# A pre-norm decoder layer on one core: the second chunk of tokens is loaded right behind the keys' weights, and products of ones stand between the last two steps of the maxima's lead

## The chip, the cores and the metric

The kernel runs on one NeuronCore of a Trainium2 chip. The metric is the device time of one execution in microseconds (us); lower is better. The profile is of one execution. In it PE is the matrix engine (TensorE), PEld its weight loads, DVE the vector engine, ACT the scalar engine, POOL the GpSimd engine, and SP the engine that issues all the DMA transfers here. L526 is line 526 of the kernel before.

## The reference

Two sequences of 2048 tokens with 512 features go through three residual sub-layers. The numbers are float32.

```python
x = x + attn(layernorm(x), W_q, W_k, W_v, W_o)         # 16 heads of 32, rotary angles on Q and K
x = x + xattn(layernorm(x), ctx, ctx)                  # gelu(x @ ctx.T) @ ctx, 77 context rows
x = x + ffn(layernorm(x), weights, scale, bias)        # x @ sign(weights).T * scale + bias, clipped at +-100

# attn, with s = 2048
Q = apply_rope(proj(W_q)); K = apply_rope(proj(W_k)); V = proj(W_v)
attn = softmax(Q @ K.T / sqrt(32))
return (attn @ V) @ W_o.T
```

## The kernel before, in words

**Two batches, two stages each.** A batch is one sequence. `project_batch` goes through its 16 chunks of 128 tokens and leaves Q, K and V in SBUF. `Attention.run` then goes through the queries in 32 units of 256 queries for four heads, eight steps a unit, and weaves the work behind attention (output product, context layer, last product) into the steps. The second batch's projection follows the first batch's attention. What is left of the last queries' work closes the kernel.

**One chunk of the projection.** The tokens come by one DMA of 256 KB (`load_x`, L76). DVE takes mean and variance (`chunk_stats`, L159 and L160). `scale_and_shift` (L168 to L171) makes the factor and the offset; its power (L169) is always on POOL, and the other three small operations are on POOL for all chunks but the very first, which has them on DVE. ACT applies factor and offset (`xn`, L183), PE transposes the result (`turn`, `pt`, L195), ACT copies it to SBUF (`xnt`, L197). PE then makes the products `pk`, `pq` and `pv` with the weights (`times`, L205). DVE rotates keys and queries by the angles (L236 to L240), POOL adds the two halves (L241), and PE transposes the sums (`ptqk`, L213).

**Where the loads stand.** All DMAs go through SP, in the order of the program. At the start these are the tokens of chunk 0, the weights of the keys, the queries and the values in four pieces of 256 KB each, the tokens of chunk 1, and the two tables of angles. Two token buffers take turns, so chunk 2's load waits until chunk 0's has been read by ACT. While the loads run, PE works through 48 products of a 128 by 128 tile of ones (`warm`, L111), whose result nobody reads.

**Who sets the order.** In the projection the order on each engine is set by a scheduler when the kernel is built; from then on each engine takes its instructions strictly in that order. At the end of the projection (from the last chunk's products on) the order on PE and DVE is the one written in the program; in the attention steps it is written by hand for all four engines.

**The maxima's lead.** The softmax needs each query's maximum over all keys before the exponentials. A step of the maxima (`maxima`) is four score products `ps` of 128 queries and 512 keys, one for each head (L526; each uses 32 of the array's 128 rows), and four reductions on DVE (L538). `lead` works off the first eleven steps, each when the block of keys that it needs is complete. The two that need the last block of keys stand back to back behind the value products of the second last chunk (`att.lead(AHEAD)`). Four PSUM buffers hold the `ps` tiles, so the second of the two waits for the first's reductions. Behind the two stand the last chunk's value products (`pv`), the last transposes of the queries, and the maxima's way into the first unit: `split_maxima` on DVE and POOL, a transpose on PE (`ptm`), a copy on DVE (`mrow`) and the first scores (`st`).

```python
        att.lead(AHEAD)                       # two steps of ps, the second waits for the reductions
        values(ch, xnt, ps_t)                 # pv of the last chunk
        transpose_qk(ch, r[:, 0], (0,))
        att.split_maxima(0)
        att.turn_maxima(0)
```

Of the kernel before, what the change touches and what calls it, by code (L numbers as in the profile page):

```python
# [9 lines left out]
F32 = mybir.dt.float32  # L10
# [6 lines left out]
P = 128  # L17
# [3 lines left out]
ND = D // P  # L21
# [6 lines left out]
WARM = 48  # L28
STEPS = NCH // 2
AHEAD = STEPS + 3  # L30
# [7 lines left out]
def decoder_layer(  # L38
# [16 lines left out]
    nc = tc.nc  # L55
# [11 lines left out]
    ps_acc = ctx.enter_context(tc.tile_pool(name="ps_acc", bufs=1, space=bass.MemoryType.PSUM))  # L67


    def tokens(rows, ch):  # L70
        return rows.rearrange("(p c) d -> c p d", c=NCH)[ch]


    def load_x(b, ch, pool=xpool):
        t = pool.tile([P, D], F32, tag="x", name=f"x_{b}_{ch}")
        nc.sync.dma_start(t, tokens(x[b], ch))  # L76
        return t

    def load_w(src, name, pieces=1):
        t = const.tile([P, ND, D], F32, tag=name, name=name)  # L80
        rows = src.rearrange("(i p) o -> p i o", p=P)
        size = ND // pieces
        for i in range(0, ND, size):
            nc.sync.dma_start(t[:, i : i + size], rows[:, i : i + size])
        return t


    def load_qkv(pieces=1):
        return [load_w(w, name, pieces) for w, name in ((wk_t, "wk"), (wq_t, "wq"), (wv_t, "wv"))]


    x_next = [load_x(0, 0)]
    qkv = load_qkv(ND)
    x_next.append(load_x(0, 1))


    def load_angles():
# [7 lines left out]
    ones_b = const.tile([P, P], BF16, tag="ones_b", name="ones_b")  # L105
    nc.vector.memset(ones_b, 1.0)


    warm = ps_acc.tile([P, P], F32, tag="acc", name="warm")
    for n in range(WARM):  # L110
        nc.tensor.matmul(warm, ones_b, ones_b, start=(n == 0), stop=(n == WARM - 1))  # L111
    ident = const.tile([P, P], F32, tag="ident", name="ident")
    make_identity(nc, ident)
    ident_b = const.tile([P, P], BF16, tag="ident_b", name="ident_b")
# [73 lines left out]
    def norm(ahead, b, ch, engine=nc.gpsimd):  # L188
        *_, xn = chunk_norm(ahead, b, ch, engine)
        return xn  # L190

    def turn(xn):
        pt = ps_t.tile([P, ND, P], F32, tag="t", name="pt")
        for i in range(ND):
            nc.tensor.transpose(pt[:, i, :], xn[:, i * P : (i + 1) * P], ident)  # L195
        xnt = work.tile([P, ND, P], F32, tag="w", name="xnt")
        nc.scalar.copy(xnt, pt)  # L197
        return xnt
# [3 lines left out]
    def project_batch(b, ahead, att, xnt, angles, wk, wq, wv):  # L202
        def times(dst, xnt, w, part=range(ND)):
            for i in part:
                nc.tensor.matmul(dst, xnt[:, i, :], w[:, i, :], start=(i == 0), stop=(i == ND - 1))  # L205

        def transpose_qk(ch, qk, which=(0, 1)):
            blk, c = divmod(ch, CPB)
            cols = slice(c * P, (c + 1) * P)
            for a in which:  # L210
                pt = ps_s.tile([P, ND, P], F32, tag="s", name="ptqk")
                for i in range(ND):
                    nc.tensor.transpose(pt[:, i, :], qk[:, a, i * P : (i + 1) * P], ident)  # L213
                (nc.vector.tensor_copy if a else nc.scalar.copy)((att.q, att.k)[a][blk][:, :, cols], pt)  # L214
            if c == CPB - 1 and 1 in which:
                att.open_block(blk)

        def values(ch, xnt, pool=None):
            pv = (pool or ps_s).tile([P, D], F32, tag="t" if pool else "s", name="pv")
            times(pv, xnt, wv)  # L220
            keep_values(ch, pv)

        def keep_values(ch, pv):
            v = kvq.tile([P, D], F32, tag=f"v{ch}", name=f"v_{b}_{ch}")
            nc.scalar.copy(v, pv)
            att.v.append(v)


        def rotate(ch, a, ps, r):
            half = [P, H, DK // 2]  # L230
            cs = angles[:, 0, ch, None, :, None].to_broadcast(half + [2])
            sn = angles[:, 1, ch, None, :].to_broadcast(half)
            pairs = ps.rearrange("p (h i t) -> p h i t", i=DK // 2, t=2)
            t1 = r[:, 0, a, :].rearrange("p (h i t) -> p h i t", i=DK // 2, t=2)
            t2 = r[:, 1, a, :].rearrange("p (h i t) -> p h i t", i=DK // 2, t=2)
            nc.vector.tensor_tensor(t1, pairs, cs, ALU.mult)  # L236
            nc.vector.scalar_tensor_tensor(
                t2[:, :, :, 0], pairs[:, :, :, 1], -1.0, sn, ALU.mult, ALU.mult
            )
            nc.vector.tensor_tensor(t2[:, :, :, 1], pairs[:, :, :, 0], sn, ALU.mult)  # L240
            nc.gpsimd.tensor_add(r[:, 0, a], r[:, 0, a], r[:, 1, a])  # L241

        held = None
        for ch in range(NCH):
            if ch == (NB - 1) * CPB:
                drain()
            blk, c = divmod(ch, CPB)
            if c == 0:
                att.q.append(kvq.tile([P, ND, BLK], F32, tag=f"q{blk}", name=f"q_{b}_{blk}"))
                att.k.append(kvq.tile([P, ND, BLK], F32, tag=f"k{blk}", name=f"k_{b}_{blk}"))  # L250
            r = big.tile([P, 2, 2, D], F32, tag="s", name="r")
            xn = norm(ahead, b, ch + 1) if ch + 1 < NCH else None
            pk = ps_t.tile([P, D], F32, tag="t", name="pk")
            pq = ps_t.tile([P, D], F32, tag="t", name="pq")
            if ch == NCH - 1:
                break
            times(pk, xnt, wk)
            rotate(ch, 1, pk, r)
            att.lead(1)
            background_between(2)  # L260
            times(pq, xnt, wq)
            rotate(ch, 0, pq, r)
            background_between(2)
            if held is not None:
                transpose_qk(*held)
            held = (ch, r[:, 0])
            xnt_next = turn(xn)
            if ch < NCH - 2:
                values(ch, xnt)
            else:  # L270
                left = xnt
            background_between(2)
            xnt = xnt_next


        ordered = tc.manual_schedule(
            engines={mybir.EngineType.PE, mybir.EngineType.DVE}
        )
        ordered.__enter__()
        times(pk, xnt, wk)  # L280
        rotate(ch, 1, pk, r)
        transpose_qk(*held)
        times(pq, xnt, wq)
        transpose_qk(ch, r[:, 0], (1,))
        rotate(ch, 0, pq, r)
        pv = ps_t.tile([P, D], F32, tag="t", name="pv")
        times(pv, left, wv, (0,))
        att.lead(1)
        times(pv, left, wv, range(1, ND))
        keep_values(ch - 1, pv)  # L290
        att.lead(AHEAD)
        values(ch, xnt, ps_t)
        transpose_qk(ch, r[:, 0], (0,))
        att.split_maxima(0)
        att.turn_maxima(0)
        ordered.__exit__(None, None, None)
        att.key_steps()
# [188 lines left out]
    def background_between(n):  # L486
        if heavy[0]:
            background(1)
            n -= 1
        background(n, light=True)  # L490

    def drain():
        while queue:
            background(1)
# [4 lines left out]
    class Attention:  # L499
# [224 lines left out]
                if n % NB == kb:  # L724
                    self.due.append((n, (0, 1, 2, 3)))

        def lead(self, steps):
            while self.due and steps > 0:
                self.maxima(*self.due.pop(0))()
                steps -= 1  # L730

# [93 lines left out]
    for b in range(B):  # L827
        att = Attention(b)
        project_batch(b, x_next, att, xnt, angles, *qkv)
        if b == 0:  # L830
            late_loads()
        load_ctx(b)
        xnt = att.run()
        if b + 1 < B:
            x_next = att.x_next
            qkv = load_qkv()
            angles = load_angles()
# [52 lines left out]
```

## Time and profile before

| What | us |
|---|---|
| median of three runs (2673.86 to 2674.93) | 2674.23 |
| the profiled execution's own time | 2675.63 |
| its span, first to last instruction | 2673.8 |
| PE busy | 2651.6 (99% of the span) |
| DVE, ACT, POOL busy | 1725.5, 1319.7, 1772.3 |
| mean granted clock of PE, as a share of the full one | 0.997 |

The span is some 1.8 us shorter than the profiled execution's time; that part lies outside the first and the last instruction. "Busy" of PE is modelled and includes waiting inside its pipeline. A row of the timeline holds start, duration, engine, line, operation, tiles and count; in brackets is the idle time of the engine before it and what ended it. "PEclk" in a table of windows is the clock that was granted to PE in that stretch, 1.00 being the full one.

### The profile page before, as it was taken

What the parts mean: (1) busy time and instruction counts of PE and PEld (TensorE: products, weight loads), DVE (VectorE), ACT (ScalarE), POOL (GpSimd) and SP (SyncE); (2) the same over time, 40 slices, a digit from 0 to 9 for tenths busy, and PEclk for the clock granted to TensorE, in tenths of its full rate; (3) what the DMA queues carried; (4) which work ended last, traced back from release to release, by engine and by line L of the source; (5) the groups of instructions that cost most, each with busy time, mean ns of one, the idle gap of its engine ahead of it and who ended that gap; (6) DMA issues with size and microseconds to landing.
All of it is one profiled execution on the core that took longest, in us unless ns stands there. A gap on an engine that the chain in (4) does not pass through costs nothing.

```text
span 2673.8 us, 70990 instructions
## 1 busy us (share of the span) xinstructions
PE 2651.6 (99%) x30548; PEld 1483.7 (55%) x30548; DVE 1725.5 (65%) x3046; ACT 1319.7 (49%) x2394; POOL 1772.3 (66%) x1925
## 2 busy tenths in 40 slices
PE   9999999999999999999999999999999999999998
PEld 4445555555555555555554455555555555555554
DVE  3447777577767676767244467766777677766654
ACT  2114555455555554545421155555555455545553
POOL 3226877578756875787643287766787578757872
PEclk9999999999999999999999999999999999999999
DMA  3010000000000100010211000000000000000100
GB/s 128 23 32 2 3 3 2 2 10 26 3 2 2 34 3 2 3 33 10 69 33 32 5 3 2 3 2 2 17 19 3 2 6 30 3 2 2 34 3 17
DMA packets 36970, 40.68 MB, mean 15 GB/s; under 512 B 19350, under 2 KB 19862, under 8 KB 36656
## 3 DMA queue, kind: packets, MB, share of 16 engines
q1 hardware_dynamic: 36656, 36.14, 4.5%
q8 instruction: 240, 3.93, 0.6%
q14 instruction: 74, 0.61, 0.1%
HBM read 27.23 MB, written 8.90 MB: 14 GB/s over the span
## 4 chain that ended last, share of the span: by engine, by line
PE 96%; POOL 2%; DVE 1%; DMA 0%; issue 0%; ACT 0%; SPq 0%; POOLq 0%; ACTq 0%
PE st L649 23%; PE acc L667 22%; PE ps L526 18%; PE acc L681 8%; PE pv L205 4%; PE po L436 4%; PE pq L205 4%; PE pk L205 4%; PE pf L415 2%; PE st L630 2%; PE pt L368 1%; PE ptqk L213 1%; PE po L462 1%; PE ph L443 1%; POOL sm L795 1%; PE pt L195 1%
## 5 line engine op out<-in xcount | busy, mean ns | idle before, releaser
L795 POOL TENSOR_TENSOR sm<-pw 128x512 f32<-128x512 f32 x1024 | 1298.8, 1274 | 537.6 <-ACT pw L793 528.9
L538 DVE TENSOR_REDUCE mx<-ps 128x1 f32<-128x512 f32 x2048 | 1313.2, 684 | 473.4 <-PE ps L526 453.6
L793 ACT ACTIVATE pw<-st 128x512 f32<-128x512 f32 x2048 | 1111.9, 595 | 892.4 <-PE ps L526 730.2
L526 PE MATMUL ps<-k,q 32*128 32x512 f32 x4096 | 1187.1, 640 | 2.8 <-DVE mx L538 2.8
L667 PE MATMUL acc<-pw,v 128*32 128x256 f32 x8192 | 655.0, 391 | 0.0
L681 PE MATMUL acc<-sm,ones 128*32 128x128 f32 x7680 | 388.3, 280 | 0.0
L667 PEld LDWEIGHTS acc<-pw,v 128*32 128x32 f32 x8192 | 161.9, 108 | 395.6 <-issue 374.5
L526 PEld LDWEIGHTS ps<-k,q 32*128 32x128 f32 x4096 | 348.8, 183 | 28.2 <-issue 13.7
L681 PEld LDWEIGHTS acc<-sm,ones 128*32 128x32 f32 x7680 | 247.2, 110 | 153.9
L649 PE MATMUL st<-q,dkk 32*128 32x256 f32 x2048 | 291.1, 400 | 0.0
L649 PE MATMUL st<-q,dkq 32*128 32x256 f32 x2048 | 291.0, 400 | 0.0
L649 PE MATMUL st<-q,dkv 32*128 32x256 f32 x2048 | 289.9, 400 | 0.0
L649 PEld LDWEIGHTS st<-q,dkk 32*128 32x128 f32 x2048 | 174.2, 184 | 85.1 <-issue 47.0
L649 PEld LDWEIGHTS st<-q,dkq 32*128 32x128 f32 x2048 | 173.8, 184 | 77.1 <-issue 57.0
L649 PEld LDWEIGHTS st<-q,dkv 32*128 32x128 f32 x2048 | 174.6, 184 | 62.7 <-issue 33.1
L704 DVE RECIPROCAL num<-num 128x64 f32<-128x64 f32 (+1 forms) x254 | 137.5, 544 | 75.5 <-ACT num L695 75.5
L241 POOL TENSOR_TENSOR r<-r 128x512 f32<-128x512 f32 x64 | 81.2, 1270 | 146.5 <-DVE r L240 145.6
L649 PE MATMUL st<-q,wrap 32*128 32x256 f32 x1024 | 144.9, 400 | 0.0
L649 PE MATMUL st<-q,k 32*128 32x256 f32 x1024 | 131.6, 374 | 0.0
L159 DVE BATCH_NORM_STATS2 st<-x 128x6 f32<-128x512 f32 x96 | 65.3, 684 | 93.4 <-DMA x<-in_x_dram 93.2
L214 ACT COPY q<-ptqk 128x512 f32<-128x512 f32 x32 | 18.8, 587 | 203.9 <-PE ptqk L213 203.9
L205 PE MATMUL pv<-wv,xnt 128*128 128x512 f32 x256 | 119.1, 608 | 0.0
(113 smaller groups left out, 2048.7 us busy)
## 6 DMA issues: line engine op xcount, KB each, us to landing
x<-in_x_dram SPq DMA_DIRECT2D x64, 256.0 KB
out_dram<-x SPq DMA_DIRECT2D x32, 256.0 KB
mrow<-rows SPq DMA_DIRECT2D x496, 0.8 KB
wk<-in_wk_t_dram SPq DMA_DIRECT2D x4, 256.0 KB
wq<-in_wq_t_dram SPq DMA_DIRECT2D x4, 256.0 KB
wv<-in_wv_t_dram SPq DMA_DIRECT2D x4, 256.0 KB
wo<-in_wo_t_dram SPq DMA_DIRECT2D x1, 1024.0 KB
wf<-in_wf_t_dram SPq DMA_DIRECT2D x1, 1024.0 KB
```

Source lines behind the costliest of these rows:

```text
L159: nc.vector.bn_stats(st, xc)
L205: nc.tensor.matmul(dst, xnt[:, i, :], w[:, i, :], start=(i == 0), stop=(i == ND - 1))
L241: nc.gpsimd.tensor_add(r[:, 0, a], r[:, 0, a], r[:, 1, a])
L436: nc.tensor.matmul(ps, ot[:, i, cols], wo[:, i, :], start=(i == 0), stop=(i == ND - 1))
L526: nc.tensor.matmul(ps, self.q[qb][self.rows[h], g, q0 : q0 + P], self.k[kb][self.rows[h], g, :], start=True, stop=True,)
L538: nc.vector.tensor_reduce(mx[:, qc, h, kb : kb + 1], ps, AX.X, ALU.max)
L649: nc.tensor.matmul(self.st[h][:, c, :], keys[r, g, kc * P : (kc + 1) * P], self.q[qb][r, g, hf * HQ : (hf + 1) * HQ], start=False, stop=Tr ...
L667: nc.tensor.matmul(acc[self.rows[h], 0, :], self.v[self.chunk(i, c)][:, d0 : d0 + DK], pw[:, h, c, :], start=(i == 0 and c == 0), stop=(i ...
L681: nc.tensor.matmul(acc[self.rows[h], 1, part], ones, sm[:, h, part], start=False, stop=(i == STEPS - 1), skip_group_check=True,)
L704: nc.vector.reciprocal(num[:, 1, k : k + size], num[:, 1, k : k + size])
L793: nc.scalar.activation(pw[:, h], self.st[h], AF.Exp, scale=SCALE)
L795: nc.gpsimd.tensor_add(sm[:, hs, :], pw[:, hs, 0, :], pw[:, hs, 1, :])
```

## The change

There are two parts. In the first, the tokens of chunk 1 are issued behind the four pieces of the keys' weights, ahead of the queries' weights; they were behind the values' weights. In the same lines the values' weights become one DMA of 1024 KB where there were four of 256 KB. In the second, `warm` becomes a function `keep_warm(n)`, and `lead` takes a second number: that many products of ones are put after each step that is not the last. Only `att.lead(AHEAD, 8)` gives it, where two steps are left, so eight products stand between these two, once in each batch. They write the PSUM buffer of the attention's sums (`ps_acc`), which is free then.

```diff
     x_next = [load_x(0, 0)]
-    qkv = load_qkv(ND)
+    qkv = [load_w(wk_t, "wk", ND)]
     x_next.append(load_x(0, 1))
+    qkv += [load_w(wq_t, "wq", ND), load_w(wv_t, "wv")]
...
-    warm = ps_acc.tile([P, P], F32, tag="acc", name="warm")
-    for n in range(WARM):
-        nc.tensor.matmul(warm, ones_b, ones_b, start=(n == 0), stop=(n == WARM - 1))
+    def keep_warm(n):
+        warm = ps_acc.tile([P, P], F32, tag="acc", name="warm")
+        for k in range(n):
+            nc.tensor.matmul(warm, ones_b, ones_b, start=(k == 0), stop=(k == n - 1))
+
+    keep_warm(WARM)
...
-        att.lead(AHEAD)
+        att.lead(AHEAD, 8)
...
-        def lead(self, steps):
+        def lead(self, steps, products=0):
             while self.due and steps > 0:
                 self.maxima(*self.due.pop(0))()
                 steps -= 1
+                if products and self.due and steps > 0:
+                    keep_warm(products)
```

Because the scheduler sets the order in the projection, the first part also moves instructions that the diff doesn't name. In the built kernels PE's order differs by the sixteen new products alone, and ACT's not at all. On DVE the head of the order is this (chunk numbers added):

```
before                                   after
statistics of chunk 0 (L159, L160)       statistics of chunk 0
variance + eps of chunk 0 (L168)         variance + eps of chunk 0
ident_b copy                             statistics of chunk 1
offset of chunk 0 (L170, L171)           ident_b copy
statistics of chunk 1                    offset of chunk 0 (L170, L171)
statistics of chunk 2 (L159)             statistics of chunk 2 (L159)
rotation of pk (L236, L237, L240)        rotation of pk
...                                      ...
```

Behind that, chunk 3's statistics stand ahead of the rotation of the first `pq` (they were behind it), POOL has chunk 3's small operations ahead of the first sum of the queries' halves, and SP has chunk 3's tokens ahead of the output weights `wo` (they were behind them).

More of the change, by code (lines that the diff above doesn't have):

```diff
@@ L85, in load_w, with load_qkv @@
         return t
-    def load_qkv(pieces=1):
-        return [load_w(w, name, pieces) for w, name in ((wk_t, "wk"), (wq_t, "wq"), (wv_t, "wv"))]
+    def load_qkv():
+        return [load_w(w, name) for w, name in ((wk_t, "wk"), (wq_t, "wq"), (wv_t, "wv"))]
     x_next = [load_x(0, 0)]
-    qkv = load_qkv(ND)
+    qkv = [load_w(wk_t, "wk", ND)]
     x_next.append(load_x(0, 1))
+    qkv += [load_w(wq_t, "wq", ND), load_w(wv_t, "wv")]
     def load_angles():
```

## The prediction

> **What bounds the kernel now.** I read the page first, then the timeline of the first 20 us, the chain of work there, the timeline around both leads, and the windows for the clock.
>
> ```profile
> PE 2651.6 (99%) x30548; PEld 1483.7 (55%) x30548; DVE 1725.5 (65%) x3046; ACT 1319.7 (49%) x2394; POOL 1772.3 (66%) x1925
> PE 96%; POOL 2%; DVE 1%; DMA 0%; issue 0%; ACT 0%; SPq 0%; POOLq 0%; ACTq 0%
> ```
>
> PE is the bound: it is busy for 99% of the span and has 96% of the chain that ends last. A microsecond in which PE gets later is a microsecond of the kernel, unless a wait behind it takes the delay up. So the whole question is what PE gains or loses in two places.
>
> The start, from the timeline:
>
> ```profile
> 3.54 0.69 DVE L159 BATCH_NORM_STATS2 st<-x 128x6 f32<-128x512 f32 x1 [2.19 <-DMA x<-in_x_dram]
> 4.27 0.18 DVE L160 BATCH_NORM_AGGREGATE stats<-st 128x2 f32<-128x6 f32 x1
> 4.49 0.15 DVE L168 TENSOR_SCALAR stats<-stats 128x1 f32<-128x1 f32 x1
> 5.38 0.16 DVE L170 TENSOR_TENSOR stats<-stats 128x1 f32<-128x1 f32 x1 [0.60 <-POOL stats L169]
> 5.82 0.81 ACT L183 ACTIVATE xn<-x,stats 128x512 f32<-128x512 f32 x1 [3.60 <-DVE stats L171]
> 6.68 0.66 PE L195 MATMUL pt<-ident,xn 128*128 128x128 f32 x4 [1.43 <-ACT xn L183]
> 7.38 0.59 ACT L197 COPY xnt<-pt 128x512 f32<-128x512 f32 x1 [0.75 <-PE pt L195]
> 8.02 3.70 PE L205 MATMUL pk<-wk,xnt 128*128 128x512 f32 x8 [0.68 <-ACT xnt L197]
> 13.51 0.69 DVE L159 BATCH_NORM_STATS2 st<-x 128x6 f32<-128x512 f32 x1 [7.78 <-DMA x<-in_x_dram]
> 16.92 0.66 PE L195 MATMUL pt<-ident,xn 128*128 128x128 f32 x4 [1.77 <-ACT xn L183]
> ```
>
> Chunk 0 goes from its statistics (3.54) to PE's first `pt` (6.68) and `pk` (8.02). Then PE waits 1.77 us for chunk 1's `pt` at 16.92, whose tokens came only at 13.5. The chain says where the tokens were:
>
> ```profile
> 3.04 4.98 DMA wq<-in_wq_t_dram
> 8.04 5.44 DMA x<-in_x_dram
> ```
>
> The fifth weight piece, issued at 3.04, landed at 8.02; SP issued chunk 1's tokens only then, and they landed at 13.48.
>
> The leads, from the timeline (first and second batch) and the windows:
>
> ```profile
> 204.11 1.14 PE L526 MATMUL ps<-k,q 32*128 32x512 f32 x8
> 206.02 2.32 PE L526 MATMUL ps<-k,q 32*128 32x512 f32 x8 [0.76 <-DVE mx L538]
> 208.27 5.40 PE L205 MATMUL pv<-wv,xnt 128*128 128x512 f32 x8
> 1531.10 2.51 PE L526 MATMUL ps<-k,q 32*128 32x512 f32 x8 [0.77 <-DVE mx L538]
> 1533.54 5.16 PE L205 MATMUL pv<-wv,xnt 128*128 128x512 f32 x8
> ```
>
> ```profile
> 3.97:7.38 3.41, 1.94 (x27) 1.53 (x24) 1.05 (x6) 0.81 (x2) 0.55 (x1) 1.00 0.97 292
> 14.21:17.62 3.41, 1.64 (x8) 0.80 (x7) 2.94 (x8) 0.81 (x2) 2.00 (x5) 1.00 0.74 274
> 205.36:208.77 3.41, 2.75 (x9) 1.18 (x10) 3.41 (x6) 0.00 (x0) 0.00 (x0) 0.99 0.00 0
> 208.77:212.18 3.41, 3.41 (x5) 1.35 (x4) 1.60 (x5) 0.00 (x0) 1.07 (x5) 0.50 0.00 0
> 1533.14:1536.56 3.42, 3.42 (x6) 1.47 (x5) 2.31 (x6) 0.00 (x0) 0.82 (x4) 0.51 0.00 0
> ```
>
> (Columns: window, length, PE, PEld, DVE, ACT, POOL busy, then the granted clock.) Behind each lead the clock is half for 3.41 us, and eight passes of `pv` take 5.2 and 5.0 us there, where `pv` elsewhere takes 3.44 (its row at 17.58 in the chain).
>
> **What the clock seems to follow.** Its changes at 3.97, 208.77, 1533.14 and 2652.72 us are whole multiples of 3.413 us apart, so I cut the trace into such windows and added up PE's work in each: a 512-column pass takes 0.43 us (3.44 over 8), a `ps` pass counts a quarter (32 of 128 rows), a transposition 0.11. The window 205.36 to 208.77 has eight `ps` passes (0.86) and one of `pv` (0.43): 1.3 us. The same sum gives 1.2 us before 1533.14 and 0.8 before 2652.72. All three were followed by half a clock. The poorest windows that kept the full clock are 14.21 to 17.62 with 1.4 us and 3.97 to 7.38 with 1.5 (1.1 of ones, 0.4 of transposes). So I put the border between 1.3 and 1.4 us.
>
> **Part 1, the start.** Chunk 1's tokens take the place of the fifth weight piece, of the same 256 KB, so I let them land at 8.02. Bounds: 3.04 + 2.82 = 5.9 (chunk 0's tokens, 0.72 to 3.54, on an empty queue) and 3.04 + 5.44 = 8.5; the row in the same place of the queue is nearest. But in the built order DVE does chunk 1's statistics ahead of chunk 0's offset, and DVE takes its work in order. What queues behind that wait is chunk 0's way to PE:
>
> - statistics 8.05, aggregate 8.78 (+0.73, as 3.54 to 4.27), the `ident_b` copy, offset at about 9.06 instead of 5.38: 3.68 us late.
> - `xn` +0.44 (5.38 to 5.82) at 9.50, `pt` +0.86 at 10.36. PE has had nothing since the ones ended at 5.26: a hole of 5.1 us, where 1.43 us were.
> - At full clock `pk` would start 1.34 later (6.68 to 8.02), at 11.70, and `pk` and `pq` with 16 passes of 0.43 (6.88) end at 18.58. Chunk 1 is long ready then (statistics at 8.05 plus the 3.4 us from 13.51 to 16.92, behind `xnt`), so its `pt` follows at once. It was at 16.92: **+1.66 us**, the vanished wait of 1.77 already in it.
> - The clock: window 3.97 to 7.38 now holds 1.1 us of ones and no `pt`, under the border; 7.38 to 10.80 nearly nothing; 10.80 to 14.21 has over 2 us. So half a clock from 7.38 to 14.21. The four transposes take 0.43 longer; `pk` starts at 12.13 and does 1.04 us of work in the 2.08 to 14.21. **+0.43 + 1.04 = +1.47 us.** Where the windows lie against the program in another execution I can't say; any place of them leaves at least one poor window in that hole. The clock's return then lies between 12.6 and 16.0, which makes the start +2.3 to +4.0.
>
> Start: **+3.13 us**. From 20 to 191 us the timeline of PE has no wait but 0.73 at 191.03, which is a copy's own time, so nothing takes the delay up.
>
> The other moves cost nothing. The queries' pieces land 0.65 later (pieces are 0.65 apart, SP's issues at 6.14, 6.79 and 7.42 waiting for them): 10.8 at the last, `pq` starts after 15. `wv` whole has landed when the same bytes were through, 13.5; `pv` needs it at 20. SP has three instructions less. The angles come at about 14; the rotation waits for `pk` until over 16. Chunk 2's load waits for ACT's reading of chunk 0 (10.3 instead of 6.6), but its place behind the angles lets it land near the old 14.9; chunk 3's leaves at 12.5 instead of 16.90, so its statistics ahead of `pq`'s rotation are ready. POOL's four small operations moved ahead of a sum take 1.3 us, and that sum is needed ten us later. If a cover failed it would be by the wait left over, under 1 us each.
>
> **Part 2, the leads.** The eight products go into PE's wait of 0.76 us (0.77): at the mean of the 48 at the start (4.22/48 = 0.088) they are 0.70 us, at most what is free, and 0.45 at the pitch of those that ran at full clock (21 in the 1 us from 4.1). Nothing else in the lead needs PE before the reductions release the second step. Cost 0; if they began late, up to 0.7 a batch. What they bring: 0.45 us of whole-array work to windows that hold 1.1 to 1.4 without it, over the border wherever the windows lie. Then `pv` takes 3.43: 5.24 - 3.43 = 1.81 in the first batch, 5.00 - 3.43 = 1.57 and 0.19 of the `ps` (2.44 to the next row against 2.25) in the second. Next late is `ptm`, which needs POOL's `first_mt` at 211.80; with `pv` done at 211.7 and four transposes it comes at 212.0. So all is kept: **-1.81 - 1.76 = -3.57 us**. If the half clock comes anyway, 0.
>
> [...]
>
> **Sum.** 2675.63 + 3.13 - 3.57 = 2675.2. That execution is 1.4 above the median of 2674.23. If the difference is what profiling costs, I should land at 2673.8; if it is that other executions had one half-clock spell less at the leads, those gain less from part 2 and all end near 2675.2. I take **2675.0**, nearer to the second, since one spell is 1.7 us and the runs differ by 1.1 among themselves.
>
> **Rivals.**
> - *B, slower: the start's loss stands alone.* The products don't hold the clock, or most executions have no half-clock spell there. For it: the border rests on five windows. Against: two of two leads show the spell. 2674.23 + 3.1 to 2675.63 + 3.1: 2677.3 to 2678.7. It decides as soon as the products add less than 0.1 us of work to a window. Chance 0.16.
> - *C, faster: the early tokens only help.* If they landed by 4.7 DVE would not be held and 1.77 would go: 2675.63 - 1.77 - 3.57 = 2670.3, or 2668.9 from the median. The earliest bound of 5.9 speaks against it. 0.06.
> - *D: the start is late, but the clock stays full.* +1.66 - 3.57: 2672.3 to 2673.7. Against: 1.1 us is under three windows that lost it. 0.08.
> - *E: at the start the clock returns a window later* (17.62): `pk` loses 2.7 instead of 1.0, +4.8; with the leads' gain 2675.5 to 2676.9, without it 2679.0 to 2680.4. 0.05.
> - *A, the forecast*: 0.65, with its own range 2673.0 to 2676.1 (the start's +2.3 to +4.0, and the two readings of the 1.4).
>
> The range 2672.5 to 2678.0 holds A, nearly all of D and half of B. 0.2%, about what a measurement of this kernel can tell from no change, is 5.3 us: below 2668.9 is only the end of C (0.01), above 2679.6 a part of B and E (0.04). So 0.95 for within it.
>
> **What would show it.** Right: DVE's second statistics at about 8.0 and ACT's first `xn` at 9.5; PE's first `pt` at 10.4 and the second at 20.0 with no wait before it; a clock of 0.50 in the stretch before 14; PEclk 1.00 behind both leads with `pv` at 3.4 us. Wrong: tokens of chunk 1 there before 6, the first `pk` at 8 as before, or a second `ps` step that starts later behind the reductions because the products are in its way.

## The result, and the profile after

The changed kernel takes 2677.51 us (median of 22 runs, 2676.00 to 2678.91), the kernel before in the same runs 2674.12 (22 runs, 2672.32 to 2675.87). The ratio is 1.0014 with a 95% interval of 1.0007 to 1.0020: slower by 3.4 us, within the 0.2% that was named as no change. The prediction was 2675.0 in a range of 2672.5 to 2678.0.

The two profiled executions alone would tell another story: 2676.00 against 2675.63. Of its 22 runs the changed kernel's profiled one is the lowest, and the profiled one of before would be the second highest among its 22. Much of the experiments is about why that is so.

The page of the changed kernel: PE is the bound as before, with the same share of the chain.

```profile
PE 2652.0 (99%) x30564; PEld 1485.2 (56%) x30564; DVE 1725.1 (65%) x3046; ACT 1318.8 (49%) x2394; POOL 1769.9 (66%) x1925
PE 96%; POOL 2%; DVE 1%; issue 0%; ACT 0%; DMA 0%; SPq 0%; POOLq 0%; ACTq 0%
```

The start, from the timeline (lines have moved by 1 to 6: statistics are L163, the offset L174 and L175, `xn` L187, `pt` L199, the products L209):

```profile
7.73 0.69 DVE L163 BATCH_NORM_STATS2 st<-x 128x6 f32<-128x512 f32 x1 [3.19 <-DMA x<-in_x_dram]
8.67 0.15 DVE L174 TENSOR_TENSOR stats<-stats 128x1 f32<-128x1 f32 x1
...
9.10 0.81 ACT L187 ACTIVATE xn<-x,stats 128x512 f32<-128x512 f32 x1 [6.88 <-DMA wq<-in_wq_t_dram]
...
9.97 1.11 PE L199 MATMUL pt<-ident,xn 128*128 128x128 f32 x4 [4.32 <-ACT xn L187]
...
11.76 5.29 PE L209 MATMUL pk<-wk,xnt 128*128 128x512 f32 x8 [0.68 <-ACT xnt L201]
...
16.88 3.60 PE L209 MATMUL pq<-wq,xnt 128*128 128x512 f32 x8
...
20.32 0.60 PE L199 MATMUL pt<-ident,xn 128*128 128x128 f32 x4
```

DVE waits 3.19 us for chunk 1's tokens with chunk 0's offset behind that wait (8.67, before 5.38). So `xn` is at 9.10, before at 5.82. (The profile names a weight's DMA as what ended ACT's wait; the order on DVE and the times say it was the offset, which ended 0.09 us before.) PE's first `pt` comes at 9.97 (6.68). The second `pt` has no wait ahead of it any more, and still stands at 20.32 where it stood at 16.92: +3.40 us. `pk` takes 5.29 us instead of 3.70, and the windows say why:

```profile
4.75:8.16 3.41, 0.89 (x15) 0.72 (x13) 0.43 (x1) 0.00 (x0) 0.50 (x1) 1.00 0.99 356
8.16:14.99 6.83, 4.35 (x8) 2.23 (x9) 1.24 (x6) 2.11 (x3) 1.26 (x4) 0.50 1.05 365
...
208.65:212.06 3.41, 3.20 (x17) 1.50 (x16) 3.41 (x6) 0.00 (x0) 0.00 (x0) 1.00 0.00 0
1533.00:1537.00 4.00, 4.00 (x13) 1.67 (x13) 4.00 (x9) 0.00 (x0) 0.00 (x0) 1.00 0.00 0
```

From 8.16 to 14.99 us the granted clock is 0.50. At both leads it is full, and there the timeline reads:

```profile
207.45 1.14 PE L530 MATMUL ps<-k,q 32*128 32x512 f32 x8
208.52 0.62 PE L113 MATMUL warm<-ones_b 128*128 128x128 bf16 x8
209.35 2.32 PE L530 MATMUL ps<-k,q 32*128 32x512 f32 x8 [0.21 <-DVE mx L542]
211.61 3.70 PE L209 MATMUL pv<-wv,xnt 128*128 128x512 f32 x8
215.15 0.60 PE L217 MATMUL ptqk<-ident,r 128*128 128x128 f32 x4
...
1532.80 2.32 PE L530 MATMUL ps<-k,q 32*128 32x512 f32 x8 [0.21 <-DVE mx L542]
1535.05 3.70 PE L209 MATMUL pv<-wv,xnt 128*128 128x512 f32 x8
1538.59 0.60 PE L217 MATMUL ptqk<-ident,r 128*128 128x128 f32 x4
```

The transposes behind `pv` stood here in the profile before:

```profile
213.51 0.60 PE L213 MATMUL ptqk<-ident,r 128*128 128x128 f32 x4
...
1538.54 0.60 PE L213 MATMUL ptqk<-ident,r 128*128 128x128 f32 x4
```

The products take 0.62 us of PE's wait and leave 0.21 of it. The second step starts 1.90 us behind the first (1.91 before, 204.11 to 206.02). `pv` takes 3.70 where it took 5.40. From the second step to the transposes behind `pv` it is 5.80 us (209.35 to 215.15) instead of 7.49, in the second batch 5.79 (1532.80 to 1538.59) instead of 7.44. The account of these two executions is then +3.40 at the start, -3.34 at the leads, and +0.3 in the last product, `pf` (8.04 us against 7.71), which had half a clock for its first 0.7 us (until 2660.32; before, the clock was full again at 2659.50, as `pf` began): together the 0.38 by which the spans differ (2674.2 against 2673.8 on the page).

### The profile page after: what moved, and what is told of

Its sections match the earlier page's. It is cut to its first block, busy times and chain, and to the rows that moved or that the text cites. A ratio compares the mean times of both kernels' runs of the same rounds, so it can differ in the third digit from the quotient of the medians.

```text
span 2674.2 us, 71017 instructions
## 1 busy us (share of the span) xinstructions
PE 2652.0 (99%) x30564; PEld 1485.2 (56%) x30564; DVE 1725.1 (65%) x3046; ACT 1318.8 (49%) x2394; POOL 1769.9 (66%) x1925
## 4 chain that ended last, share of the span: by engine, by line
PE 96%; POOL 2%; DVE 1%; issue 0%; ACT 0%; DMA 0%; SPq 0%; POOLq 0%; ACTq 0%
PE st L653 23%; PE acc L671 22%; PE ps L530 18%; PE acc L685 8%; PE pq L209 4%; PE po L440 4%; PE pk L209 4%; PE pv L209 4%; PE pf L419 2%; PE st L634 2%; PE pt L372 1%; PE ptqk L217 1%; PE po L466 1%; PE ph L447 1%; POOL sm L801 1%; PE pt L199 1%
## 5 line engine op out<-in xcount | busy, mean ns | idle before, releaser
L163 DVE BATCH_NORM_STATS2 st<-x 128x6 f32<-128x512 f32 x96 | 65.2, 683 | 90.4 <-DMA x<-in_x_dram 90.1
L209 PE MATMUL pk<-wk,xnt 128*128 128x512 f32 x256 | 117.1, 600 | 2.1 <-ACT xnt L201 2.1
```

The lines of the kernel that those rows point to most:

```text
L163: nc.vector.bn_stats(st, xc)
```

## The experiments

The kernels of the first eight experiments had eleven runs each and are compared with the kernel before in the same set of runs (33 runs a set); that had a median of 2674.14 us in the first set and 2673.20 in the second. The last four are single executions. The theory under test was the prediction's: DVE's wait for the early tokens and the half clock behind it cost over 3 us, and the products win back what the half-clock spells at the leads cost.

**The early tokens alone.**

```diff
-        att.lead(AHEAD, 8)
+        att.lead(AHEAD)
```

> The changed kernel without the eight products between the last two steps of the lead; the early tokens and the one piece of wv stay. My theory: the start costs about 3.4 us (second pt at about 20.3 instead of 16.9, first pk at about 11.8) and the leads lose the clock as often as before, so the kernel is 3.4 us (2.5 to 4.5) above the kernel before and up to 1 us above the changed kernel's usual time; any profile that shows 0.50 behind a lead shows pv at 5.0 to 5.3 us there. Rival, that the products are what costs (they stand on PE): then this one is no slower than the kernel before, and 3 us under the changed kernel.

2677.61 us, ratio to before 1.0017 (1.0008 to 1.0025). So the loss belongs to the first part, and products as the cost are ruled out. Four of the eleven runs stood apart at 2679.1 to 2680.3, above the highest of the changed kernel. The profile of one of the others has full clock at both leads without any product; its second `pt` is as late as the changed kernel's.

```profile
20.98 0.60 PE L199 MATMUL pt<-ident,xn 128*128 128x128 f32 x4
...
212.28 3.70 PE L209 MATMUL pv<-wv,xnt 128*128 128x512 f32 x8
```

**The products alone.**

```diff
-    qkv = [load_w(wk_t, "wk", ND)]
+    qkv = [load_w(w, name, ND) for w, name in ((wk_t, "wk"), (wq_t, "wq"), (wv_t, "wv"))]
     x_next.append(load_x(0, 1))
-    qkv += [load_w(wq_t, "wq", ND), load_w(wv_t, "wv")]
```

> The kernel before with the eight products alone; all loads stand where they stood before. My theory: they fit into PE's wait of 0.76 us and keep the clock full behind both leads in every execution, so 0 to 3.5 us are gained, depending on how many half-clock spells an execution had: the highest times come down most (before ranged over 3.5 us, this one should range over 2 us or less), and the median falls by about 0.9 us (0.3 to 1.8). pv behind the leads 3.4 us, second step of ps at 206.0 as before. Rival, that products on PE cost: second step of ps starts later than 206.1 and the median rises by up to 1.4 us. Rival, that they do nothing: same range and median, and a profile with 0.50 behind a lead.

2673.10 us, 1.04 under the kernel before; the interval of the ratio, 0.9988 to 1.0006, does not exclude no gain. The second step is not pushed back by the products: it stands 1.90 us behind the first, which is at 205.98 here because the start was late (below).

```profile
207.05 0.62 PE L112 MATMUL warm<-ones_b 128*128 128x128 bf16 x8
207.88 2.32 PE L529 MATMUL ps<-k,q 32*128 32x512 f32 x8 [0.21 <-DVE mx L541]
210.14 3.70 PE L208 MATMUL pv<-wv,xnt 128*128 128x512 f32 x8
```

The range of 2672.3 to 2675.3 is wider than I expected, by one run, the profiled one. It has full clock at both leads, but a half-clock spell from 18.45 to 21.86 us, behind PE's wait for chunk 1's tokens at the start, which the products don't reach.

```profile
17.09 0.66 PE L198 MATMUL pt<-ident,xn 128*128 128x128 f32 x4 [2.07 <-ACT xn L186]
17.59 5.29 PE L208 MATMUL pv<-wv,xnt 128*128 128x512 f32 x8
```

The kernel before has the same wait at that place (1.77 and 2.22 us in two of its three profiles), so some of its slower runs may have this spell and none at a lead. The other ten runs here lie below 2673.8; of the 33 of the kernel before in the same set 17 lie above that.

**The early tokens, with chunk 0's offset ahead on DVE.** The order of DVE is written by hand for the first two chunks' statistics.

```diff
+    first = tc.manual_schedule(engines={mybir.EngineType.DVE})
+    first.__enter__()
     xnt = turn(norm(x_next, 0, 0, nc.vector))
...
             xn = norm(ahead, b, ch + 1) if ch + 1 < NCH else None
+            if b == 0 and ch == 0:
+                first.__exit__(None, None, None)
```

> The changed kernel with one thing more: DVE's order at the start is fixed so that chunk 0's offset (L174, L175) stands ahead of chunk 1's statistics, as it did before. Nothing else moves. My theory: DVE's wait for the early tokens was the whole loss. First xn at 5.7, first pk at 8.0, second pt at about 15.0 with no wait ahead of it, 1.9 us earlier than in the kernel before and 5.3 earlier than in the changed kernel; where the clock is half in the first pk, up to 1.7 of that is lost. Median 1 to 2.8 us under the kernel before, 4.5 to 6 under the changed kernel. Rival, that the transfers cost (queries' weights later, wv as one piece): first pk or pq waits for a DMA and the median stays 2 us or more above the kernel before.

2671.11 us, ratio to before 0.9990 (0.9981 to 0.9999), 6.4 under the changed kernel. From its timeline:

```profile
5.88 0.81 ACT L187 ACTIVATE xn<-x,stats 128x512 f32<-128x512 f32 x1 [3.67 <-DVE stats L175]
8.09 3.70 PE L209 MATMUL pk<-wk,xnt 128*128 128x512 f32 x8 [0.68 <-ACT xnt L201]
8.23 0.69 DVE L163 BATCH_NORM_STATS2 st<-x 128x6 f32<-128x512 f32 x1 [2.44 <-DMA x<-in_x_dram]
...
15.06 0.60 PE L199 MATMUL pt<-ident,xn 128*128 128x128 f32 x4
...
15.49 3.60 PE L209 MATMUL pv<-wv,xnt 128*128 128x512 f32 x8
```

The tokens are there at 8.2, about as in the changed kernel (7.7 to 8.2 in its three profiles), and the second `pt` follows `pq` at 15.06 without a wait; `pv` follows without one too. Against the changed kernel only two instructions (chunk 1's statistics) have another place on DVE. So the transfers cost nothing that shows: the whole loss hangs on what stands behind DVE's wait.

**A longer run of ones at the start**, with DVE's wait left in.

```diff
-WARM = 48
+WARM = 128
```

> The changed kernel with 128 products of ones at the start where it has 48, so that PE is busy nearly until the late first pt. My theory of the clock: the hole behind the ones halves the clock, which is 2 of the 3.4 us at the start. Filled, the first pk runs at full clock: first pt near 10.0 (up to 0.9 later where the ones run at half clock for longer), second pt at 18.2 to 19, and 1 to 2.5 us less than the changed kernel, yet still 0.5 to 2 above the kernel before. Rival, that the whole loss is DVE's wait and the clock takes no part: same time as the changed kernel within 0.5 us.

2674.74 us, ratio to before 1.0004 (0.9995 to 1.0013), 2.8 under the changed kernel.

```profile
1.04 9.62 PE L113 MATMUL warm<-ones_b 128*128 128x128 bf16 x128 [1.04 <-DVE ones L121]
10.53 0.66 PE L199 MATMUL pt<-ident,xn 128*128 128x128 f32 x4
11.86 3.70 PE L209 MATMUL pk<-wk,xnt 128*128 128x512 f32 x8 [0.68 <-ACT xnt L201]
...
18.83 0.60 PE L199 MATMUL pt<-ident,xn 128*128 128x128 f32 x4
```

`pk` is as late as in the changed kernel (the tokens came 0.56 us later in this execution, at 8.29 for 7.73) and runs at full speed. So the clock takes part, and the two shares of the loss can be estimated from the medians: what is left against the kernel with the products alone is DVE's wait, 2674.74 - 2673.10 = 1.64 us; what went is the clock, 2677.51 - 2674.74 = 2.8 us. The rows agree for the clock: from DVE's statistics of the early tokens to the second `pt` it is 10.54 us here, 12.59 in the changed kernel's profile above, and 12.90 and 13.51 in its two others (below), so 2.0, 2.4 and 3.0 us.

**The products' worth, with the start in order.** Three sisters of the kernel with chunk 0's offset first ran in one set: without products in the lead, with two, and with eight and `wv` in four pieces.

```diff
-        att.lead(AHEAD, 8)
+        att.lead(AHEAD)
```

> The changed kernel with chunk 0's offset ahead of chunk 1's statistics on DVE, and without the products in the lead. My theory: it differs from its sister with eight products (median 2671.1) by the half-clock spells at the leads alone: none, one or two of 1.75 us, so its lowest times stay near 2670.7, its median is 0.5 to 1.8 us higher and its highest times reach 2674 or more. Against the kernel before it shows the early tokens' worth alone: 1.5 to 2.5 us less. Rival, that the products don't act: same median and same highest time as the sister, within 0.3 us.

```diff
-        att.lead(AHEAD, 8)
+        att.lead(AHEAD, 2)
```

> As the kernel with chunk 0's offset first, but two products of ones between the steps of the lead where there are eight. They add 0.11 us of work to windows that hold 1.1 at the poorest, and by the border of 1.3 to 1.4 us that is not enough. My theory: spells at the leads as with none, a little rarer: median 0.3 to 1.5 us above the sister with eight (2671.1), highest times above 2673.5. Rival, that any activity in the wait keeps the clock, whatever its amount: no spell, median within 0.3 us of 2671.1.

```diff
-    qkv += [load_w(wq_t, "wq", ND), load_w(wv_t, "wv")]
+    qkv += [load_w(wq_t, "wq", ND), load_w(wv_t, "wv", ND)]
```

> As the kernel with chunk 0's offset first, but the values' weights come in four pieces of 256 KB again and not as one DMA. My theory: the first pv needs them at 15.5, 2 us behind the last byte, so one or four makes no difference: median within 0.3 us of 2671.1, second pt at 15.0 followed at once by pv. Rival, that one large piece is late: pv waits for it in the kernel with one piece and not here, and this one is faster by that wait.

| In the lead | median | range | ratio to before |
|---|---|---|---|
| none | 2670.81 | 2670.33 to 2672.23 | 0.9992 (0.9983 to 1.0001) |
| two | 2670.99 | 2669.97 to 2672.44 | 0.9991 (0.9982 to 1.0000) |
| eight, `wv` in four pieces | 2670.91 | 2669.96 to 2672.33 | 0.9991 (0.9982 to 1.0000) |

By time the rivals win here: eight products are worth nothing that these runs can show, where I expected 0.5 us or more. That `wv` came in four pieces makes no difference either, which was expected. The same comparison with the start left late gives as little by the medians: 2677.61 without products, 2677.51 in the changed kernel. Medians of runs that fall into two groups jump; by the means the products bring 0.7 us there, 0.6 in the kernel with the products alone against the kernel before, and 0.1 here, each with a standard error of 0.3 to 0.4. The traces still show the spells. In the kernel with two products one lead of the two lost the clock, `pv` takes 5.39 us there:

```profile
1526.36 0.29 PE L113 MATMUL warm<-ones_b 128*128 128x128 bf16 x2
1527.19 2.32 PE L532 MATMUL ps<-k,q 32*128 32x512 f32 x8 [0.55 <-DVE mx L544]
1529.44 5.39 PE L209 MATMUL pv<-wv,xnt 128*128 128x512 f32 x8
```

**Sixty products at the start**, with chunk 0's offset first and eight products in the lead.

```diff
-WARM = 48
+WARM = 60
```

> The changed kernel with chunk 0's offset ahead of chunk 1's statistics on DVE, and 60 products of ones at the start where it has 48. Its sister with 48 ran from 2670.6 to 2672.7 in two groups 1.7 us apart. My theory: the upper group had a half-clock spell behind the hole between the ones and the first pt (1.3 us), and 0.67 us more of ones fill it up: one group near 2670.7, median 2670.5 to 2671.1. Rival, that the two groups come from the kernel's end: two groups as before, median within 0.3 us of 2671.1. Rival, that more ones push the first pt back: first pt later than 6.9 and the median up by as much.

2670.41 us, ratio 0.9990 (0.9982 to 0.9999), and one group from 2670.0 to 2671.1; the sisters with 48 have a second group 1.5 us higher (three to five of eleven runs). First `pt` at 6.74, not later, and without a wait ahead of it:

```profile
6.74 0.66 PE L199 MATMUL pt<-ident,xn 128*128 128x128 f32 x4
```

The mean granted clock tells the groups apart: 0.997 in all seven upper runs of the two sisters with eight products, 0.998 in their lower ones and in all eleven here. So the upper group is a half-clock spell, and that filling the start's hole removes it speaks for that hole and against the kernel's end. No profile caught an execution of that group with eight products. DVE's order is not quite the same either: chunk 2's statistics stand behind the rotation of `pk` here and ahead of it in the sisters; PE's rows from the first `pt` to 22 us agree with the first sister's to 0.01 us. This kernel has the lowest median of the study, 2.8 us under the kernel before; against its sisters the 0.4 to 0.5 us are not clear of noise.

**Both kernels again**, for profiles with the clock's windows in other places.

> The changed kernel once more, for a second profile of the same program. The windows of the clock lie elsewhere against the program each time. If a pass counts by its work, not by its time, a window at half clock needs some 2.7 us of busy PE to bring the full clock back, so it returns between 14 and 17.4 us; the second pt then stands at 20.3 plus half of what the return is later than 14.99, plus what the tokens land later than 7.7. No half clock at the leads. If the return is by time, as my prediction had it, it can come from 12.6 on and never after 16.0.

> The changed kernel a third time, with the same expectation: the clock's return between 14 and 17.4 us, second pt at 20.3 plus half of what the return is later than 14.99, plus what the tokens land later than 7.7. No half clock at the leads.

> The kernel before once more. My theory: the profiled execution that the prediction was summed on had the most half-clock spells that the leads can have, two. Another one has none, one or two; with none its time is near 2672.5, with one near 2674.3. A spell follows a lead exactly when the window that covers it has less than 1.3 us of work. Rival, that both spells belong to every execution: two again, at about 2675.

> The kernel before a third time, with the same expectation: none, one or two spells at the leads, and a time near 2672.5, 2674.3 or 2675.6 accordingly.

The changed kernel had 2676.80 and 2677.70 us. The clock came back at 15.98 and 17.31 us, and the second `pt` stood at 21.00 and 21.66, each 0.2 under what was expected. The second of them:

```profile
10.39 1.07 PE L199 MATMUL pt<-ident,xn 128*128 128x128 f32 x4 [4.05 <-ACT xn L187]
12.14 6.25 PE L209 MATMUL pk<-wk,xnt 128*128 128x512 f32 x8 [0.68 <-ACT xnt L201]
21.66 0.60 PE L199 MATMUL pt<-ident,xn 128*128 128x128 f32 x4
```

```profile
10.48:13.89 3.41, 2.73 (x6) 1.42 (x7) 0.00 (x0) 1.30 (x2) 0.18 (x1) 0.50 0.96 344
13.89:17.31 3.42, 3.42 (x5) 1.35 (x4) 0.69 (x1) 0.00 (x0) 0.00 (x0) 0.50 0.97 301
```

In the first of these windows PE is busy for 2.73 us, but at half clock that is 1.2 us of work, and the clock stays half for another window. By time, as I had it in the prediction, it would have come back at 13.89. The window that brought it back in the changed kernel's first profile held 1.6 us of work:

```profile
11.58:14.99 3.41, 3.23 (x4) 1.52 (x5) 0.46 (x1) 0.83 (x2) 0.00 (x0) 0.50 1.06 328
```

The ones at the start come nearest to the border: in the kernel with two products they run from 1.04 us on, at half pace, and the clock is full from 3.71, after 2.67 us, which by that pace is 1.3 us of work. (The 48 weight loads of the ones take 5.04 us, 0.105 each, in the changed kernel's last profile, where all stand ahead of the full clock; the eight at a lead take 0.45, 0.056 each.)

The kernel before had 2672.79 and 2673.33 us, and neither execution had a half-clock spell at a lead. The first had one at the start:

```profile
8.08 5.40 PE L205 MATMUL pk<-wk,xnt 128*128 128x512 f32 x8 [0.68 <-ACT xnt L197]
...
17.03 0.66 PE L195 MATMUL pt<-ident,xn 128*128 128x128 f32 x4
```

There `pk` takes 5.40 us, and the second `pt` is hardly later than in the first profile (16.92): in this execution the wait for the tokens took the spell up.

**The leads of all profiles together.** I summed PE's work in the clock's windows as in the prediction; that a `ps` pass counts a quarter there is an estimate of mine from its 32 of 128 rows, which no run tests by itself.

| Products between the steps | leads profiled | followed by half a clock | poorest window (us of work) |
|---|---|---|---|
| none (before three times, e1, e6) | 10 | 2 | 1.20 |
| two (e7) | 2 | 1 | 1.19 |
| eight (changed kernel three times, e2, e3, e4, e5, e8) | 16 | 0 | 1.52 |

At the leads the windows that lost the clock had 1.19, 1.20 and 1.28 us. Of the poor ones that kept it one, the second batch's in the last profile of the kernel before, had 1.24 (1.30 if each pass is spread over its time), the next 1.39. So the border lies near 1.3 us, not sharper than 0.1 by this sum, in which some records are missing. That lead breaks the rule that I had put down for it, a spell exactly below 1.3, by the first way of counting and keeps it by the second.

## Why the prediction was right or wrong

**The place** was right, the balance was not. My sum had the leads give back more than the start costs (3.57 against 3.13); by the medians the start costs 4.4 us (2677.51 - 2673.10) and the leads give back 1.0 (2674.14 - 2673.10), or, by the kernel with the tokens alone, 3.5 and 0.1. The range held the time by its width: 2677.51 lies outside the forecast's own part, 2673.0 to 2676.1, and in that of rival B, to which I gave 0.16. As forecast, no wait stands ahead of the second `pt`, `xn` is at 9.10 (forecast 9.50, the tokens came 0.3 us earlier than I took), `pt` at 9.97 (10.36), and nothing takes the delay up on the way to the first lead, which is 3.34 us late (207.45 against 204.11).

**DVE's wait**, "+1.66 us" at full clock, was right: 1.64 by the medians of the kernel with 128 ones and the one with the products alone.

**The clock at the start** was right in kind and too small. The step that failed is "+0.43 + 1.04 = +1.47 us" with its bounds, "between 12.6 and 16.0": it let the clock come back as soon as a window had 1.35 us of busy PE. A pass at half clock takes twice its time (in the changed kernel's first profile the weight loads of `pk` stand 0.85 us apart ahead of 14.99 and 0.43 behind it), and all profiles fit if it counts by its work: the window then needs some 2.7 us. The three profiles of the changed kernel show 14.99, 15.98 and 17.31. The term is 2.8 us by the medians, 2.0 to 3.0 by the rows of the three profiles. Rival E, to which I gave 0.05, was this in part: a return one window later.

**The leads**, "-1.81 - 1.76 = -3.57 us", measured -1.69 and -1.65 in the pair of profiles. The mechanism held: 16 leads with eight products and no spell. What failed is the step from this one execution to the median. It had two spells, and the kernel before ran at all times between 2671.7 and 2676.6 us; of its 66 runs in the two sets 34 were under 2673.6, 25 between that and 2675.1, and 7 above. The mean granted clock agrees that these are half-clock spells: 0.998 in 25 of the 34, 0.997 in the other 9 and in all 32 above. Where a spell stood in a run without a profile isn't known; the start can have one too, as in two of the profiles (8.39 to 11.81 us in the kernel before, 18.45 to 21.86 with the products alone). The profiled one, at 2675.63, belongs to the last kind. I had named this ("if it is that other executions had one half-clock spell less at the leads") and my 2675.0 still leaves the products 2.4 us (2674.23 + 3.13 - 2675.0), more than the one spell of 1.7 that a run of the middle group has. Rival B said what came out for the time, at 2677.3 to 2678.7, and half of why: of its two conditions the first, that the products don't hold the clock, did not come true, the second, that most executions have no spell at the leads, holds for about half of them by their times. By the medians the products bring 1.0 us in one pair of kernels, 0.1 in a second (2677.61 without, 2677.51 with) and 0.1 with the wrong sign in a third (2670.81 without, 2670.91 with), none of them clear of noise.

**What was costed at nothing** held: the products stay within the wait, later pieces of `wq` and `wv` are waited for by nobody (`pq` follows `pk` at 16.88 us without a wait, `pv` follows the second `pt` at 20.75), and one piece or four makes no difference (0.9990 of the kernel before with one, 0.9991 with four).

**What the early tokens could have brought**, the 1.77 us of PE's wait, is there once DVE is not held: 2673.10 with the products alone, 2671.11 with the tokens too, 1.99 us less.

**The clock's changes and PE's waits.** Within one profile all changes of the clock are whole multiples of 3.413 us apart (in the changed kernel's first profile 2 of them from 8.16 to 14.99 and 773 from there to 2653.49), and the first full clock comes anywhere from 3.7 to 7.1 us (in the kernel with two products and in the changed kernel's last profile). The length of PE's wait alone does not tell whether the clock is lost: the changed kernel lost it behind a wait of 4.3 us at the start, the kernel with the products alone behind one of 2.07 us, and at the leads, where no wait is longer than 0.77 us, two of ten without products lost it.

## What to carry to other kernels

When a load is moved ahead, look at the order that a scheduler then gives the engines that consume it: an instruction that waits for the new data may now stand ahead of work that was ready. Here DVE worked in that order: it waited 3.19 us, and chunk 0's offset behind that wait came 3.3 us later (8.67 for 5.38). Before a sum is made against one profiled execution, compare its time with the spread of the runs: a term that belongs to that execution alone (here up to two spells of half clock, 1.7 us each) must not be counted as the kernel's. And a hole on PE can cost twice, as it did here, by its length (1.64 us by the medians) and by the slow work behind it (2.8). Products of ones filled it at no cost where they fitted into the wait (at the lead the second step stands 1.90 us behind the first with eight of them, 1.91 without): at the start they brought 2.8 us with the late tokens, at the leads no gain clear of noise.

## What the runs showed of the hardware that was not expected

- One border, near 1.3 us of work in a window of 3.41 us, fits both the loss of the full clock and its return. At half clock that takes twice the busy time: with 2.73 us busy and 1.2 us of work (10.48 to 13.89) it stayed half, and with 3.23 us and 1.6 (11.58 to 14.99 in the changed kernel's profile) it came back. At full clock a window with 1.64 us busy and 1.4 of work (14.21 to 17.62 in the kernel before) kept it. A border of its own for the return is not excluded.
- The windows do not lie at the same place against the program in all profiles (the first full clock came at 3.7 to 7.1 us), and the kernel before lost the clock at both leads in one profile and at none in two others. The leads that lost it, in all profiles, had 1.19 to 1.28 us of work in the window ahead, those that kept it 1.24 or more. One and the same kernel has groups of times some 1.2 to 1.7 us apart: 34, 25 and 7 of 66 runs in the kernel before, the lowest group mostly at a mean clock of 0.998 (25 of 34), the others all at 0.997. The groups run into each other in the second set.
- A spell can follow a stretch without any idle time over 0.8 us, where PE uses a quarter of its rows (32 of 128 in the `ps` products): 3 of the 12 leads with none or two products.
